# The sum of eight scan results, and x times D, on VectorE instead of GpSimd, under another table of slots

## The chip, the cores and the metric

The kernel runs on one core of a Trainium2 chip. A core has five instruction queues: TensorE (PE in the profile; its weight loads are PEld), VectorE (DVE), ScalarE (ACT), GpSimd (POOL) and SyncE (SP), which here issues nearly all DMA transfers. The metric is device time in microseconds, start to end of one execution; the times given are medians of several runs on the chip. All data is fp32.

## The reference

Eight images of 56 × 56 pixels with 192 channels go through two layers, each with a residual connection.

Layer 0 normalises the image in groups of channels, projects it three times to 576 channels (p, q, v, each through silu), multiplies q by v, convolves the product along rows and along columns with long learned filters, multiplies the sum by p and projects back.

Layer 1 is a two-dimensional selective scan. Cut to what matters:

```
xz = gn(x) @ W_in.T ; xc, z = split(xz)          # 384 + 384 channels
xc = silu(depthwise_conv3x3(xc))
xs = eight orders of the pixels of xc            # K = 8 directions
h[t] = exp(delta[t] * A) * h[t-1] + delta[t] * xs[t] * B[t]     # 16 states a channel
out_y[k] = sum over states of h * C  +  D[k] * xs
y = y0 + y1 + ... + y7                           # each put back into pixel order
y = layernorm(y) * silu(z)
x = x + y @ W_out.T
```

Since D times the input is added for every direction at the same pixel, the kernel adds (sum of the eight D) times xc once per pixel.

## The kernel before

Layer 0 runs first, for all images (its part ends some 3.4 ms into the span). Then layer 1 alternates between a stage that this case calls the stage between images and the scan of one image. The loop `for b in range(-1, B)` has nine such stages: the first only brings image 0 in, the next seven carry image b out and bring image b + 1 in, and the last only carries image 7 out. Eight scans lie between them.

A scan (lines 720 to 1130) is 9600 / 8 = 1200 units of a recurrence over 1024 columns on VectorE (L973), each followed by a multiplication by C on GpSimd (L986) and by transposes on TensorE (L1095) that also sum over the states. The scan's order is written out by hand. Its results go to DRAM, `ytd[b]`, eight results of 384 channels for every pixel; x itself lies in `xrd[b]`.

The stage between images works in tiles of 448 pixels, seven per image. Two streams run in it:

- X, the next image (class `Next`): `load`, `normed` (L458 on VectorE), `project` (L465 on TensorE, L486 on ScalarE), `conv` in three parts (nine taps for three blocks of channels; block 1 on TensorE with diagonal weights, L501, blocks 0 and 2 on VectorE, L505 for the first tap and L503 for the rest), `silu` (L513, ScalarE), `turn` and `away` (transposes and a store of x by pixel), `rows` (L527 on TensorE: the projections that the scan needs, stored by L541), `half` (copies of x into the other orders). For two of the four groups of rows the projection reads the image by columns, so it needs the whole image; those are stream C and come after the last tile of X.
- Y, the image that was scanned (class `Tile`): `load`, `pairs`, `total`, `root`, `scales`, `scaled`, `turn_back`, `normed`, `gate`, `gated`, `finish`. A tile has four parts of 112 pixels. Their inputs are brought ahead by `load_y` (stream L): `yr`, the first four results, `yc`, the other four, and `xty`, x; six buffers each. `pairs(i)` multiplies x by the summed D (L600) and adds the last four results to the first four (L601). `total(i)` adds on: four to two (L608), two to one (L609), plus x times D (L610), and takes the statistics (L611, L612). `root`, `scales`, `scaled` finish the layer norm on ScalarE and VectorE (L616, L620, L622, L628), `turn_back` transposes to channels by rows (L641, L646), `gate` projects z and applies silu (L465, L662), `gated` multiplies (L665), `finish` projects by W_out (L671), adds the residual (L678) and stores (L679).

The order is given by the table PROGRAM. For each step s the table is gone through; an entry such as `('Y', 1, 'scaled')` does that method of tile s − 1 − lag, where the Y stream runs 4 steps later than X (`LAG`), so that X's first four tiles are begun alone. This is the order in which the program names the instructions, and with it their priority. In this stage no order is written out by hand: the framework's planner lays the instructions of each engine by their priorities, its own estimate of durations and when their inputs are due. In the trace VectorE's order therefore departs from the table's. Once laid, each engine's queue is in order, and SyncE's too: a store that is not ready holds the loads behind it.

Of the kernel before, what the change touches and what calls it, by code (L numbers as in the profile page):

```python
# [40 lines left out]
ALU = mybir.AluOpType  # L41
# [5 lines left out]
L = HW * HW  # L47
C = 192
# [23 lines left out]
NR = 5  # L72
AHEAD = 12
LAG = 4
PROGRAM = [('Y', 2, 'gated'), ('Y', 1, 'root'), ('L', 0, '', 1), ('X', 0, 'normed'), ('C', 2, 'rows', 0, 3), ('X', 2, 'conv', 0), ('X', 0, 'project'), ('Y', 1, 'scales'), ('X', 2, 'conv', 1), ('X', 2, 'conv', 2), ('X', 3, 'turn'), ('L', 0, '', 2), ('Y', 0, 'pairs', 1), ('Y', 2, 'finish'), ('Y', 0, 'pairs', 2), ('Y', 1, 'scaled'), ('Y', 0, 'pairs', 0), ('X', 3, 'away'), ('Y', -1, 'pairs', 3), ('Y', 1, 'turn_back'), ('X', 3, 'half', 0), ('Y', 0, 'total', 3), ('Y', 0, 'load'), ('Y', 0, 'total', 1), ('Y', 0, 'normed'), ('C', 2, 'rows', 1, 3), ('L', 0, '', 0), ('Y', 0, 'total', 2), ('X', 3, 'rows', 0), ('Y', 0, 'total', 0), ('C', 2, 'rows', 1, 2), ('X', 3, 'rows', 1), ('L', 1, '', 3), ('Y', 1, 'gate'), ('X', 4, 'half', 1), ('X', -3, 'load'), ('C', 2, 'rows', 0, 2), ('X', 2, 'silu')]
SIZES = (8, 8, 8, 8, 8, 8, 2)
assert sum(SIZES) == NC

# [14 lines left out]
def conv_kernel(ctx: ExitStack, tc: tile.TileContext, a: dict, out: bass.AP):  # L93
    nc = tc.nc
# [337 lines left out]
    for b in range(-1, B):  # L432
        with ExitStack() as st:
# [18 lines left out]
            if norm:  # L452
                wout = one.tile([128, NB, C], F32, name="wout")
                dsb = one.tile([J, DI], F32, name="dsb")
# [128 lines left out]
            class Tile:  # L583
# [9 lines left out]
                def pairs(self, i):  # L593
                    if i == 0:
                        self.st = wk.tile([J, 4, 6], F32, name="yst")
                        self.mv = wk.tile([J, 4, 2], F32, name="ymv")
                        self.yk = {}
                    j = 4 * self.t + i
                    yk, yc, xt = yks[j]
                    nc.gpsimd.tensor_tensor(xt, xt, dsb, ALU.mult)  # L600
                    nc.gpsimd.tensor_tensor(yk[:, 0:4], yk[:, 0:4], yc, ALU.add)  # L601

                def total(self, i):
                    j = 4 * self.t + i
# [78 lines left out]
            X = [Next(t) for t in range(NT)] if more else []  # L683
            Y = [Tile(t) for t in range(NT)] if norm else []
# [18 lines left out]
            for s in range(NT + 12):  # L703
                for stream, late, name, *args in PROGRAM:
                    t = s - late
# [510 lines left out]
```

## Time and profile before

| | |
|---|---|
| median of 3 runs | 28777.4 us (28766.57 to 28782.69) |
| profiled execution | 28792.29 us, span 28790.5 us |
| busy in the span: PE, DVE, ACT, POOL | 26720.9, 25230.4, 21866.3, 22107.1 us |
| stages that carry out and bring in, seven of them | 376.0 to 384.4 us each |
| first stage (in only), last stage (out only) | 226.2 us, 254.1 us |
| DVE busy, POOL busy in the second of the seven | 269.5, 176.3 us |
| L601 on POOL, whole run | 224 times, 905.0 us busy |

A row of the groups gives line, engine, operation, names and shapes, count, busy time, mean duration of one in ns, and the idle time of that engine just before it. A row of the view by source line gives the shortest, median and longest duration in ns. A row of the waits gives who waited for whom, the total in us, how often, and the longest. A row of the timeline gives start and duration in us. Windows are in us from the start of the span. Busy time on an engine is the time from an instruction's start to its end, whatever it did in between.

### The profile page before, as it was taken

The numbers are of one execution on the slowest core, as the hardware profiler recorded it, in microseconds if no ns is written. First come the engines' busy times: TensorE is split into PE (matmuls) and PEld (weight loads), VectorE is DVE, ScalarE is ACT, GpSimd is POOL, SyncE is SP. The second block draws the span as 40 slices with busy tenths as digits, with TensorE's granted clock in tenths as the row PEclk, the third lists the DMA queues.
The fourth block names the chain that finished last, engine by engine and source line by source line (L and its number), as shares of the span: only waits on it lengthen the run. The fifth ranks groups of instructions, "written<-read, shape, count | busy, mean of one in ns | idle before, by whom it ended". The sixth has DMA issues, their size and how long they took to land. (4 is left out here: it accounts for less than half of the span.)

```text
span 28790.5 us, 459134 instructions
## 1 busy us (share of the span) xinstructions
PE 26720.9 (93%) x148912; PEld 15134.0 (53%) x148912; DVE 25230.4 (88%) x16084; ACT 21866.3 (76%) x58050; POOL 22107.1 (77%) x10384
## 2 busy tenths in 40 slices
PE   7999999998999899989999899989998999989997
PEld 4555555554555455544555455545555455545554
DVE  3444489998999899998999899989999899989998
ACT  2333288986998588867889588858997688858886
POOL 0000089987999699987999699979998799969998
PEclk9999999999999999999999999999999999999998
DMA  4222266666666676666666666666666766667666
GB/s 99 57 54 64 62 174 170 171 170 188 172 172 171 174 184 170 171 173 184 173 172 171 182 177 170 172 177 180 171 174 167 190 171 171 171 174 184 170 173 176
DMA packets 5889181, 4641.39 MB, mean 161 GB/s; under 512 B 3814944, under 2 KB 5216000, under 8 KB 5878336
## 3 DMA queue, kind: packets, MB, share of 16 engines
q1 hardware_dynamic: 5853632, 4604.79, 62.1%
q8 instruction: 1189, 19.48, 0.3%
q10 hardware_dynamic: 33152, 7.23, 0.2%
q14 instruction: 1208, 9.90, 0.1%
HBM read 3848.20 MB, written 911.76 MB: 165 GB/s over the span
## 5 line engine op out<-in xcount | busy, mean ns | idle before, releaser
L986 POOL TENSOR_TENSOR hc<-h,cbt 128x1008 f32<-128x1008 f32 x9600 | 20579.1, 2165 | 1708.0 <-DVE h L973 1249.0
L973 DVE TENSOR_TENSOR_SCAN h<-da,bx 128x1024 f32<-128x1024 f32 x9600 | 21122.8, 2264 | 523.3 <-ACT bx L969 492.4
L937 ACT ACTIVATE da<-delta,A_logs 128x252 f32<-128x252 f32 (+1 forms) x39936 | 16821.6, 488 | 771.4 <-DVE h L973 765.6
L958 PE MATMUL bx<-bd,dus 63*128 63x504 f32 x19200 | 10567.5, 635 | 404.5 <-DVE h L973 403.2
L958 PE MATMUL bx<-bd,dut 63*128 63x504 f32 x19200 | 10566.7, 635 | 352.0 <-DVE h L973 328.8
L1095 PEld LDWEIGHTS yps<-ident,hc 128*126 128x126 f32 x76800 | 8311.6, 140 | 3790.2 <-issue 3436.3
L1095 PE MATMUL yps<-ident,hc 128*126 128x128 f32 x76800 | 9449.9, 276 | 210.5 <-POOL hc L986 160.6
L958 PEld LDWEIGHTS bx<-bd,dus 63*128 63x128 f32 x19200 | 2876.6, 186 | 2149.6 <-DVE h L973 1348.6
L958 PEld LDWEIGHTS bx<-bd,dut 63*128 63x128 f32 x19200 | 2876.5, 186 | 2087.4 <-DVE h L973 1234.4
L451 POOL MEMSET xp<- 128x58 f32 x96 | 10.4, 196 | 3417.4 <-DMA x1d<-acc 3417.0
L969 ACT COPY bx<-h 128x16 f32<-128x16 f32 x9408 | 1631.3, 173 | 1081.8 <-PE bx L958 1014.0
L601 POOL TENSOR_TENSOR yr<-yr,yc 112x1536 f32<-112x1536 f32 x224 | 905.0, 4040 | 864.9 <-DMA yc<-yt 547.7
L810 PE MATMUL pd<-dt,dtw 13*128 13x504 f32 x2304 | 1311.6, 649 | 121.9 <-DMA dt<-pxd 41.6
L1122 ACT COPY yt<-yps 126x256 f32<-126x256 f32 x2400 | 859.0, 358 | 579.3 <-PE yps L1095 556.8
L849 PEld LDWEIGHTS pt<-ident,delta 128*128 128x128 f32 x4800 | 503.0, 142 | 1242.3 <-issue 1004.4
L857 DVE TENSOR_TENSOR dut<-pt,xt 128x384 f32<-128x384 f32 x1600 | 850.3, 531 | 337.1 <-DMA bd<-bd 153.9
L849 PE MATMUL pt<-ident,delta 128*128 128x128 f32 x4800 | 886.5, 294 | 34.7 <-ACT delta L825 27.9
L810 PEld LDWEIGHTS pd<-dt,dtw 13*128 13x128 f32 x2304 | 344.7, 187 | 1004.8 <-issue 523.2
L261 ACT ACTIVATE q<-pp,q_b 128x448 f32<-128x448 f32 (+1 forms) x280 | 177.3, 633 | 900.3 <-PE pp L257 900.3
L527 PE MATMUL mm<-xp,pxw 128*128 128x448 f32 x1344 | 823.4, 760 | 0.0
L503 DVE SCALAR_TENSOR_TENSOR acc<-xp,conv_w,acc 128x448 f32<-128x448 f32 x896 | 769.5, 908 | 12.9 <-ACT xp L486 10.5
L319 DVE TENSOR_TENSOR acc<-acc,po 96x896 f32<-96x896 f32 x280 | 303.3, 1083 | 522.3 <-PE po L312 521.8
(126 smaller groups left out, 15384.3 us busy)
## 6 DMA issues: line engine op xcount, KB each, us to landing
cbt<-cd SPq DMA_DIRECT2D x1536, 1008.0 KB
bd<-bd SPq DMA_DIRECT2D x3200, 256.0 KB
dus<-dut SPq DMA_DIRECT2D x3200, 96.0 KB
yt<-ys SPq DMA_DIRECT2D x256, 1176.0 KB
xt<-xt SPq DMA_DIRECT2D x3104, 96.0 KB
ys<-yt SPq DMA_DIRECT2D x9408, 31.5 KB
yr<-yt SPq DMA_DIRECT2D x224, 672.0 KB
yc<-yt SPq DMA_DIRECT2D x224, 672.0 KB
```

The lines of the kernel that those rows point to most:

```text
L527: nc.tensor.matmul(ps, pxw[:, d, g], x[:, t * RT : (t + 1) * RT], start=(d == 0), stop=(d == NB - 1),)
L601: nc.gpsimd.tensor_tensor(yk[:, 0:4], yk[:, 0:4], yc, ALU.add)
L810: nc.tensor.matmul(self.pd[:, : self.n], weights[self.k][:, d * 128 : (d + 1) * 128], self.dt, start=True, stop=True,)
L849: nc.tensor.transpose(self.pt[:, d * 128 : (d + 1) * 128], self.delta[:, d, first : first + 2].rearrange("p c t -> p (c t)"), ident,)
L857: nc.vector.tensor_mul(dut, self.pt[:, :DI], self.xt[p])
L937: yield nc.scalar.activation(da[:, : self.nc, n, 1:], src, AF.Exp, scale=an[:, G.k, self.d, n : n + 1],)
L958: nc.tensor.matmul(self.bx[:, r, :, 1:], G.dut[p][q ^ r ^ int(G.rev)][rows, self.d * 128 : (self.d + 1) * 128], G.bd[p][rows, q, :, :W], s ...
L969: nc.scalar.copy(self.bx.rearrange("p r n t -> p (r n) t")[:, :, 0], src)
L973: nc.vector.tensor_tensor_scan(self.h.rearrange("p n t -> p (n t)"), das[self.P.buf][:, self.slot].rearrange("p n t -> p (n t)"), self.bx. ...
L986: nc.gpsimd.tensor_tensor(hc, h, self.G.cb[self.c // 2][:, :, q * W : (q + 1) * W], ALU.mult)
L1095: nc.tensor.matmul(yps[:, t // 4 % 2, t // 2 % 2], lhsT=hcs[t // 2][:, n].rearrange("p c t -> p (c t)"), rhs=ident, start=(n == 0), stop=( ...
L1122: nc.scalar.copy(y, yps[:, s // 4 % 2])
```

## The change

The two instructions of `pairs` are issued on VectorE instead of GpSimd, with the same operands:

```
-                    nc.gpsimd.tensor_tensor(xt, xt, dsb, ALU.mult)
-                    nc.gpsimd.tensor_tensor(yk[:, 0:4], yk[:, 0:4], yc, ALU.add)
+                    nc.vector.tensor_mul(xt, xt, dsb)
+                    nc.vector.tensor_add(yk[:, 0:4], yk[:, 0:4], yc)
```

After it GpSimd has nothing to do between images but a few memsets.

The table PROGRAM has the same 38 entries with the same delays, in another order:

```
-PROGRAM = [('Y', 2, 'gated'), ('Y', 1, 'root'), ('L', 0, '', 1), ('X', 0, 'normed'), ('C', 2, 'rows', 0, 3), ('X', 2, 'conv', 0), ('X', 0, 'project'), ('Y', 1, 'scales'), ('X', 2, 'conv', 1), ('X', 2, 'conv', 2), ('X', 3, 'turn'), ('L', 0, '', 2), ('Y', 0, 'pairs', 1), ('Y', 2, 'finish'), ('Y', 0, 'pairs', 2), ('Y', 1, 'scaled'), ('Y', 0, 'pairs', 0), ('X', 3, 'away'), ('Y', -1, 'pairs', 3), ('Y', 1, 'turn_back'), ('X', 3, 'half', 0), ('Y', 0, 'total', 3), ('Y', 0, 'load'), ('Y', 0, 'total', 1), ('Y', 0, 'normed'), ('C', 2, 'rows', 1, 3), ('L', 0, '', 0), ('Y', 0, 'total', 2), ('X', 3, 'rows', 0), ('Y', 0, 'total', 0), ('C', 2, 'rows', 1, 2), ('X', 3, 'rows', 1), ('L', 1, '', 3), ('Y', 1, 'gate'), ('X', 4, 'half', 1), ('X', -3, 'load'), ('C', 2, 'rows', 0, 2), ('X', 2, 'silu')]
+PROGRAM = [('X', 0, 'normed'), ('Y', 2, 'gated'), ('X', 2, 'conv', 0), ('X', 0, 'project'), ('C', 2, 'rows', 0, 3), ('Y', 0, 'pairs', 1), ('Y', 1, 'root'), ('X', 2, 'conv', 1), ('X', 3, 'turn'), ('Y', 1, 'scales'), ('X', 2, 'conv', 2), ('Y', 2, 'finish'), ('X', 3, 'away'), ('X', 2, 'silu'), ('L', 0, '', 2), ('Y', 0, 'pairs', 2), ('L', 0, '', 1), ('Y', 0, 'pairs', 0), ('Y', 0, 'total', 1), ('Y', 1, 'scaled'), ('Y', 1, 'turn_back'), ('Y', 0, 'load'), ('L', 0, '', 0), ('Y', 0, 'total', 3), ('Y', 0, 'total', 2), ('Y', -1, 'pairs', 3), ('C', 2, 'rows', 1, 3), ('X', 3, 'rows', 0), ('X', 3, 'rows', 1), ('C', 2, 'rows', 1, 2), ('Y', 1, 'gate'), ('Y', 0, 'total', 0), ('C', 2, 'rows', 0, 2), ('X', 3, 'half', 0), ('L', 1, '', 3), ('X', 4, 'half', 1), ('X', -3, 'load'), ('Y', 0, 'normed')]
```

`nc.vector.tensor_mul` and `tensor_add` are the two-operand product and sum on VectorE, as used in `total`. Line numbers do not move: L600 and L601 are the same two statements before and after.

## The prediction

> **What bounds the kernel now.** The page's slices first: VectorE is lowest, and TensorE stays high, wherever two scans meet, once per image. The windows then split one of these stages, the second of the seven that carry one image out and the next one in, at the end of the last scan, the first convolution, the last convolution, the end of the last projection, and the first scan. Columns: stretch and length, then busy us and instruction count of TensorE, its weight loads, VectorE, ScalarE, GpSimd; the granted TensorE clock; DMA share; GB/s.
>
> ```profile
> 9590.40:9612.00 21.60, 3.00 (x20) 2.36 (x18) 5.24 (x11) 0.74 (x2) 3.41 (x13) 0.58 0.82 257
> 9612.00:9785.10 173.10, 130.63 (x355) 66.32 (x356) 169.09 (x220) 57.41 (x106) 96.86 (x29) 0.85 0.68 186
> 9785.10:9940.00 154.90, 148.47 (x361) 59.65 (x359) 93.60 (x108) 60.23 (x112) 70.93 (x28) 0.98 0.71 215
> 9940.00:9968.20 28.20, 15.52 (x27) 5.10 (x27) 1.60 (x4) 16.98 (x36) 5.09 (x13) 0.58 0.57 112
> ```
>
> Part A (173.1 us) is VectorE's: 169.1 busy, TensorE idle 42.5. Part B (154.9) is TensorE's: idle 6.4, VectorE idle 61. The first and last pieces, 50 us, are loads and the way into the scan; the change touches neither. GpSimd bounds no part.
>
> Next, what VectorE does in A. The groups of that stage (count, busy us, mean ns, idle before):
>
> ```profile
> L503 DVE SCALAR_TENSOR_TENSOR acc<-xp,conv_w,acc 128x448 f32<-128x448 f32 x112 | 102.1, 961 | 0.2
> L608 DVE TENSOR_TENSOR yr<-yr 112x768 f32<-112x768 f32 x28 | 39.6, 1418 | 0.0
> ...
> L505 DVE TENSOR_SCALAR acc<-xp,conv_w 128x448 f32<-128x448 f32 x14 | 11.2, 817 | 1.4 <-ACT xp L486 1.4
> ```
>
> The same convolution line runs in the very first stage too, where there is no image to carry out and no GpSimd add (min/median/max ns, from the view by source line), and there it never waits:
>
> ```profile
> L503 DVE SCALAR_TENSOR_TENSOR acc<-xp,conv_w,acc x112: 670/678/686, 3444.7 to 3534.4; 128x448 f32<-128x448 f32 x112
> L505 DVE TENSOR_SCALAR acc<-xp,conv_w x14: 439/446/453, 3444.3 to 3527.0; 128x448 f32<-128x448 f32 x14
> ```
>
> And the timeline of the middle stage shows what stretches it: a 0.68 us step that starts 0.25 us after a GpSimd add ends with it, and a GpSimd multiply of usually 1.37 us that lasts 17.48 while VectorE runs its steps back to back.
>
> ```profile
> 9618.46 3.50 POOL L601 TENSOR_TENSOR yr<-yr,yc 112x1536 f32<-112x1536 f32 x1 [24.55 <-DMA xty<-xr]
> 9618.71 3.73 DVE L503 SCALAR_TENSOR_TENSOR acc<-xp,conv_w,acc 128x448 f32<-128x448 f32 x1
> ...
> 9640.85 17.48 POOL L600 TENSOR_TENSOR xty<-xty,dsb 112x384 f32<-112x384 f32 x1
> ```
>
> So each engine stands while the other holds something. "Busy" on VectorE in A holds waiting.
>
> **The waiting that goes.** In A, busy less count times the unblocked duration: L503 112 × (961 − 678) ns = 31.7 us; L505 14 × (817 − 446) = 5.2; L608 19.5 busy for 14, less 14 × 0.942 = 6.3; L610 10.0 for 13, less 13 × 0.546 = 2.9; L609 8.2 for 14, less 14 × 0.543 = 0.6; L458 12.6 for 17, less 17 × 0.504 = 4.1. Sum 51 us of 173. The same sum in B (L608 6.9, L609 11.0, L610 8.6, L458 7.3, L622 1.8) gives 36, under TensorE's cover.
>
> **The work that comes.** The multiply has the shape of L609 and L610: 0.56 us. The 112×1536 add has no VectorE row. From 384 to 768 columns (L609 0.557, L608 0.946) the slope is 1.01 ns a column; from 384 to L665's 1344 (1.557) 1.04. That gives 1.72 to 1.76 us; I take 1.74. Together 2.30, and 2.14 in a back-to-back queue, where each record overlaps the next by 0.08. All 28 cost 60 us a stage. On GpSimd the same pairs are busy 112.5 + 56.6 us; that goes and nobody queues for it.
>
> **Rule against row.** The Trainium skill (Perfetto Trace Analysis, Optimizing Scalar/DVE Operations) says that where VectorE is saturated, work may be moved off it, even to GpSimd, and warns that the shared port can spoil this. By its first half the change is wrong: 14 to 17 pairs × 2.14 = 30 to 36 us added to the engine that bounds A, some +230 us over seven stages. The rows answer with the 51 us of standing. The skill's SBUF — State Buffer (Who interferes with whom) states the mechanism: a VectorE instruction with two SBUF inputs, or in a two-port mode, and a GpSimd one that reads SBUF exclude each other whole. L503 and L505 above behave so. I take the rows: −51 + 30 to 36.
>
> **Where it ends.** In A as it stands 14 pairs and 13 totals complete. If the moved pairs keep that pace, A loses 51 − 30 = 21 us; if by the end of the convolution everything the table puts ahead is also done (four tiles and the first pair of the fifth, 17), 51 − 36 = 15. I take 18. Then TensorE, at 130.6 of a 155 us part, has 24 idle instead of 42; it cannot be squeezed evenly, so I let it give back 4. Part B keeps its length: its TensorE work is the same, and its 36 us of VectorE waiting less some 26 for the other 12 pairs was hidden behind 61 us of idleness. So 14 us a stage, 98 for seven.
>
> The first stage has no pairs: 0, with ±5 for the new order. In the last stage, which only carries out, VectorE is 179.5 of 254 busy, of which L609 28 × (1852 − 557) = 36 and L608 and L610 38 more are waiting, plus 44.6 idle at L608 for GpSimd. VectorE's sum alone would fall by 74 + 45 − 60 = 59. But loads there keep the DMA share near 1.0 for 160 us and the first pair waits for its first load: between 0 and 30, nearer the loads' bound: 10.
>
> **The table.** Its slots keep every lag except for order inside a slot: conv and projection of a tile come earlier against the sums, silu moves from the slot's end ahead of them, the normalised x for the gate goes last, pair 3 later. In the trace VectorE's order departs from the table anyway: L608 of the first tile at 9636.1 lies between convolution steps. So the planner that orders this stage will lay it anew. Bounds: from −10 us a stage (silu earlier shortens ScalarE's wait for L503) to +10 (a load behind a store); centre 0. A store does hold loads: SyncE's own waits in A, and GpSimd's, are
>
> ```profile
> SPq L679 <- DVE x L678: 32.5, 1, 32.5
> ...
> POOL yr L601 <- DMA yc<-yt: 39.4, 7, 33.2
> ...
> POOL xty L600 <- DMA xty<-xr: 13.5, 1, 13.5
> ```
>
> The moved queue matters here. GpSimd's waits cost nothing today, since nothing else stands behind them. After the change a pair that waits for its load holds VectorE, and behind it the convolution steps, silu on ScalarE, and then turns and projections on TensorE. SyncE gets no new DMA; its buffer of yc comes free when VectorE, not GpSimd, is through the add.
>
> Sum against the profiled execution (span 28790.5, 28792.3 with what lies around it): −98 − 10 = −108, so 28684. The median of the runs stands 15 lower, 28777.4; the forecast for it is 28669, say 28670.
>
> **Rivals.** *VectorE waits for loads (slower).* The place is A: the 33.2 us wait before the fifteenth pair and the 13.5 us one at the sixth multiply become VectorE's, with convolution behind. 46.7 − 18 = +29 a stage, seven stages and −10: about +190 if both are taken whole; it decides from 18 us a stage on. For it: SyncE's queue is in order and the loads do stand behind an unready store for 32.5 us. Against: that store waits for VectorE itself, which would get to it sooner; and the planner may put late pairs behind the convolution. Half exposed, it is +5 a stage, +25 in all. I take +90 as its middle.
>
> *Hidden anyway (same).* A ends 18 us earlier, but B starts with loads that were issued no earlier, at the DMA share of 0.9 to 1.0 seen in its middle, and the last output tile ends when it did. For it: the last finish (L678) ends only 4 us before the last projection, so the output stream is nearly co-critical. Against: DMA share over A is 0.68, with room to load sooner. It gives 28777 ± 50.
>
> *The change doesn't do what it says:* VectorE could still stand without GpSimd. The first stage's L503, 670 to 686 ns, speaks against that; I leave it no chance of its own.
>
> **How the numbers follow.** Some 0.2% (57 us) is what a measurement of this kernel can tell from no change. The likeliest case (0.55) is 28670, from 28560 (A loses 21, TensorE gives nothing back, the table gives 6, the last stage 30) to 28715. Hidden anyway: 0.15, 28720 to 28830. Loads hold VectorE, or the new order costs as much: 0.30, 28835 to 28970, middle 28870. Leaving about 1 in 10 out at each end gives 28560 to 28890. Faster 0.55, same 0.15, slower 0.30.
>
> **What would show it.** Right: L503 near 0.68 us mean in every stage, L601 on VectorE near 1.74, GpSimd empty between scans; A near 155 us, B near 155. Wrong: idle time of VectorE before L600 or L601 ended by a DMA in A, over 18 us a stage (the slower rival); A shorter and B longer by as much (hidden); L503 still stretched (the lock is not it); an add far above 1.76 us.

## The result, and the profile after

The changed kernel takes 28503.07 us (median, 28486.33 to 28506.23), before 28771.99 in the same comparison: the ratio is 0.9905, 95% interval 0.9889 to 0.992. The direction was forecast; the size, 269 us, is two and a half times the 108 us forecast and lies below the range.

In the profiled executions the span falls from 28790.5 to 28504.0 us, by 286.5. Cut at the stages: the seven that carry out and bring in fall from 379.6 to 341.7 us in the mean, 265 together; the last from 254.1 to 241.2, 13; the part up to the first scan by 6; the eight scans by 2. So the change acts where it was put, and in each of the seven stages it gives 37.9 us instead of 14.

The windows of the changed kernel's second such stage, cut at the same four events as before (start, first projection, last convolution, last projection for the scan, first scan; columns as before):

```profile
9547.70:9569.50 21.80, 2.32 (x20) 1.84 (x18) 5.14 (x12) 0.74 (x2) 3.40 (x13) 0.69 0.81 256
9569.50:9729.50 160.00, 150.76 (x456) 77.34 (x456) 154.63 (x264) 67.44 (x123) 0.00 (x0) 0.97 0.87 239
9729.50:9860.90 131.40, 119.44 (x258) 45.65 (x258) 77.32 (x122) 51.03 (x94) 0.00 (x0) 0.95 0.72 207
9860.90:9888.60 27.70, 15.73 (x27) 5.17 (x27) 1.57 (x3) 16.54 (x34) 5.09 (x13) 0.57 0.53 108
```

Head and tail stay at 22 and 28 us. Part A goes from 173.1 to 160.0, part B from 154.9 to 131.4. VectorE is still full in A, but TensorE, which was idle for 42 of 173 us there, is now idle for 9 of 160, and does 456 matmuls in A instead of 355. Of the 714 matmuls of A and B, 258 instead of 359 are left for B (a row can count a matmul that lies across a cut twice).

VectorE's groups of that stage:

```profile
L503 DVE SCALAR_TENSOR_TENSOR acc<-xp,conv_w,acc 128x448 f32<-128x448 f32 x112 | 68.6, 671 | 0.2
L601 DVE TENSOR_TENSOR yr<-yr,yc 112x1536 f32<-112x1536 f32 x28 | 48.9, 1747 | 1.3 <-DMA yc<-yt 1.3
L608 DVE TENSOR_TENSOR yr<-yr 112x768 f32<-112x768 f32 x28 | 26.1, 941 | 0.0
L600 DVE TENSOR_TENSOR xty<-xty,dsb 112x384 f32<-112x384 f32 x28 | 15.2, 543 | 0.0
```

The convolution step is back at 671 ns from 961, the first sum at 941 from 1418. The add costs 1747 ns, forecast 1740; the multiply 543, forecast 560. And VectorE waits for loads before its pairs for 1.3 us in the whole stage, where GpSimd had waited 74.4 us for yc.

### The profile page after: what moved, and what is told of

It is laid out like the page before. It is cut to its first block, busy times and chain, and to the rows that moved or that the text cites. A ratio compares the mean times of both kernels' runs of the same rounds, so it can differ in the third digit from the quotient of the medians.

```text
span 28504.0 us, 458613 instructions
## 1 busy us (share of the span) xinstructions
PE 26664.6 (94%) x148912; PEld 15113.4 (53%) x148912; DVE 25001.0 (88%) x16532; ACT 21872.4 (77%) x58050; POOL 20753.0 (73%) x9936
## 5 line engine op out<-in xcount | busy, mean ns | idle before, releaser
L527 PE MATMUL mm<-xp,pxw 128*128 128x448 f32 x1344 | 798.9, 745 | 2.4 <-ACT px L539 2.4
L819 ACT COPY delta<-pd 128x504 f32<-128x504 f32 x1152 | 646.1, 561 | 117.2 <-PE pd L810 97.9
```

Source lines behind the costliest of these rows:

```text
L527: nc.tensor.matmul(ps, pxw[:, d, g], x[:, t * RT : (t + 1) * RT], start=(d == 0), stop=(d == NB - 1),)
L819: nc.scalar.copy(self.delta[:, d, :, :W], self.pd[:, : self.n].rearrange("p (c t) -> p c t", t=W))
```

## The experiments

In all of them a stage is cut at the same events; A and B in the text are means over the seven stages, and the rows show the second. For the kernels above A and B are 172.5 and 156.6 before and 158.4 and 132.9 after. An instruction that waits inside its own busy time is said to stand.

### The move or the table

Two parts were changed at once. The first kernel moves the engine under the old table:

```
-                    nc.gpsimd.tensor_tensor(xt, xt, dsb, ALU.mult)
-                    nc.gpsimd.tensor_tensor(yk[:, 0:4], yk[:, 0:4], yc, ALU.add)
+                    nc.vector.tensor_mul(xt, xt, dsb)
+                    nc.vector.tensor_add(yk[:, 0:4], yk[:, 0:4], yc)
```

> The two pair instructions on VectorE under the old table. If the port is the cause (theory P), L503 falls to 0.68 us mean in every stage and the seven stages fall from about 379 to 340-350 us: 200 to 280 us of the 269 in all. If the table's order is the cause (theory T), L503 falls too, but the stages stay within 10 us of 379: less than 80 us in all, the shorter first part being given back in the second.

The second has the new table alone:

```
-PROGRAM = [('Y', 2, 'gated'), ('Y', 1, 'root'), ('L', 0, '', 1), ('X', 0, 'normed'), ...
+PROGRAM = [('X', 0, 'normed'), ('Y', 2, 'gated'), ('X', 2, 'conv', 0), ('X', 0, 'project'), ...
```

> The pairs stay on GpSimd, the new table orders the stage. Theory P: L503 stays near 0.96 us and the seven stages stay at 370 to 385 us, within 60 us of before in all. Theory T: the stages fall by 20 us or more each, 150 us or more in all, with L503 still stretched. If each gives part (both under 200 us), the two act together: the sum of both gains against 269 us says whether they add.

The move alone: 28518.38 us, ratio to before 0.9905 (0.9888 to 0.9922). The table alone: 28824.24 us, 1.0012 (1.0003 to 1.0022), slightly slower than before. The move makes the whole gain: beside the kernel before, measured with it, it saves 270 us, and the whole change 269. What the new order adds to it can't be told from no effect; without it the order costs 36 us. The convolution step of the move alone, then of the table alone:

```profile
L503 DVE SCALAR_TENSOR_TENSOR acc<-xp,conv_w,acc 128x448 f32<-128x448 f32 x112 | 68.8, 677 | 0.2
```

```profile
L503 DVE SCALAR_TENSOR_TENSOR acc<-xp,conv_w,acc 128x448 f32<-128x448 f32 x112 | 103.5, 970 | 0.8 <-ACT xp L486 0.5
```

The windows of parts A and B, in the same order:

```profile
9576.10:9732.70 156.60, 137.57 (x407) 70.99 (x408) 147.92 (x253) 63.34 (x115) 0.00 (x0) 0.91 0.92 252
9732.70:9874.50 141.80, 136.81 (x309) 52.61 (x307) 84.77 (x133) 55.32 (x102) 0.00 (x0) 0.98 0.60 184
```

```profile
9621.00:9795.90 174.90, 137.83 (x382) 69.67 (x382) 170.66 (x220) 59.58 (x109) 97.73 (x30) 0.84 0.69 190
9795.90:9954.50 158.60, 145.52 (x332) 57.68 (x332) 84.23 (x109) 58.11 (x108) 63.57 (x26) 0.96 0.73 203
```

In the mean, the move alone brings A to 153.1 and B to 142.1 us; the table then puts 49 more matmuls into A (456 after 407), and A is 5 us longer and B 9 shorter. In the last stage the table costs something in these profiles: 219.8 us under the old one, 241.2 under the new one.

### Is it the port, or the hand-over?

With the pairs on VectorE two things are gone: GpSimd beside VectorE, and VectorE's waiting for results that GpSimd delivers. This kernel brings back only the first:

```
                     nc.vector.tensor_add(yk[:, 0:4], yk[:, 0:4], yc)
+                    idle = wk.tile([J, 4, DI], F32, name="idle", bufs=1)
+                    nc.gpsimd.tensor_tensor(idle, yc, yc, ALU.add)
```

> The changed kernel, and beside each pair of adds on VectorE a GpSimd add of 1536 columns of yc to itself, into a tile that nobody reads. Nothing waits for it except the buffer of yc. If the two engines exclude each other (theory P), L503 goes back to 0.85-0.95 us mean, the first part of a stage grows by 25-40 us and the time to 28700-28800 us, about that of before. If the gain came from VectorE no longer waiting for GpSimd's results (theory H, the hand-over), L503 stays at 0.67 and the time within 60 us of the changed kernel, 28500-28560.

28844.07 us, 1.0022 (1.0013 to 1.0032) of before: the gain is gone and a little more. Stages of 383.6 us in the mean, A 192.5, B 142.0; the last stage, where the add runs too, takes 278.7. A grows by 34.1 us and VectorE's busy time in it by 34.3. The add also holds the buffer of yc longer, but VectorE waits for no load before its pairs (0.0 in the row of L601 below), so late loads are not the cause. So GpSimd's presence is enough; the hand-over is not needed. The expectation for L503 failed, though. The groups, of VectorE and of GpSimd (from L608 on, line numbers are two higher here: L610 is the sum L608):

```profile
L503 DVE SCALAR_TENSOR_TENSOR acc<-xp,conv_w,acc 128x448 f32<-128x448 f32 x112 | 68.6, 670 | 0.2
L601 DVE TENSOR_TENSOR yr<-yr,yc 112x1536 f32<-112x1536 f32 x28 | 51.4, 1836 | 0.0
L610 DVE TENSOR_TENSOR yr<-yr 112x768 f32<-112x768 f32 x28 | 33.8, 1216 | 0.0
L600 DVE TENSOR_TENSOR xty<-xty,dsb 112x384 f32<-112x384 f32 x28 | 31.4, 1120 | 0.0
...
L458 DVE TENSOR_SCALAR x1n<-x,gstat 96x448 f32<-96x448 f32 x14 | 13.8, 1009 | 0.0
```

```profile
L603 POOL TENSOR_TENSOR idle<-yc 112x1536 f32<-112x1536 f32 x28 | 146.8, 5242 | 159.8 <-DMA yc<-yt 147.7 <-DMA pxd<-px 11.0
```

The standing is carried by the sums, the multiply and the normalisation, and by GpSimd itself (5.24 us in the mean, shortest 2.75, longest 19.81), not by the convolution. It is not that GpSimd's adds fell elsewhere. In the seven stages 24 of the 196 began during an L503; each of these 24 took over 4.5 us, while the longest L503 took 0.69. In the kernel before 66 of 196 began there, only 13 of these took over 4.5 us, and 110 of the 784 L503 took over 0.9. The two adds differ in their operands (yr and yc into yr before, yc twice into a third tile here); why one held the convolution up and the other gave way to it is not shown.

### Does any GpSimd work do it?

```
+                    idle = wk.tile([J, 4, DI], F32, name="idle", bufs=1)
+                    for _ in range(3):
+                        nc.gpsimd.memset(idle, 0.0)
```

> The changed kernel, and beside each pair three GpSimd memsets of 1536 columns (about 1.4 us each), which write the on-chip memory and read none of it. If exclusion needs a GpSimd read against a VectorE step with two inputs (theory P, as the Trainium skill's SBUF page has it), L503, L608 to L610 keep their durations; only the steps with one input in the two-port mode (L505, L458) can be stretched, at most 35 of them a stage: 0-8 us a stage, 28505-28565 us. If any GpSimd work excludes VectorE, the time goes to 28700-28850 as with the add.

28626.68 us, 0.9946 (0.9931 to 0.9961): 123 us of the gain lost, twice the most that was expected. The groups say which steps stand:

```profile
L503 DVE SCALAR_TENSOR_TENSOR acc<-xp,conv_w,acc 128x448 f32<-128x448 f32 x112 | 68.6, 670 | 0.2
L601 DVE TENSOR_TENSOR yr<-yr,yc 112x1536 f32<-112x1536 f32 x28 | 48.9, 1746 | 0.5 <-DMA yc<-yt 0.5
...
L458 DVE TENSOR_SCALAR xnext<-xnext,gstat 96x448 f32<-96x448 f32 x14 | 20.4, 1494 | 15.5 <-DMA xnext<-x1d 15.5
...
L614 DVE BATCH_NORM_STATS2 yst<-ysum 112x6 f32<-112x384 f32 x28 | 14.8, 546 | 0.1
...
L505 DVE TENSOR_SCALAR acc<-xp,conv_w 128x448 f32<-128x448 f32 x14 | 12.4, 901 | 0.0
...
L458 DVE TENSOR_SCALAR x1n<-x,gstat 96x448 f32<-96x448 f32 x14 | 9.3, 688 | 0.0
```

The two-input steps shown are untouched: L503 670 ns, L601 1746, as without memsets. Of the steps with one input the TENSOR_SCALAR ones are stretched: L458 to 1494 and 688 ns from 504 or less, L505 to 901 from 446, against a memset's 1.42 us. The statistics (L611, here L614), with one input too, stay at 546. That is the distinction the Trainium skill draws (SBUF — State Buffer, Who interferes with whom): two SBUF inputs contend only with a GpSimd instruction that reads SBUF, a two-port mode, which TENSOR_SCALAR can enter, with any, and other one-input steps with none. The durations agree with it; which mode a step ran in is not in the trace. The size was missed because the memsets wait for nothing and crowd into A (none is left for B): there the three lines L458 (twice) and L505 stand for 14 × 0.99 + 14 × 0.18 + 14 × 0.46 = 23 us, which make the stage 17.5 us longer.

### Which part pays

The forecast took waiting in B as hidden by VectorE's 61 idle us. The same GpSimd add was put beside the first four tiles only, then beside the last three only, in the seven stages:

```
+                    if more and self.t < 4:       # the other kernel: self.t >= 4
+                        idle = wk.tile([J, 4, DI], F32, name="idle", bufs=1)
+                        nc.gpsimd.tensor_tensor(idle, yc, yc, ALU.add)
```

> The GpSimd add beside the pairs of the first four of the seven output tiles only (most of them run before the last convolution), in the seven stages that carry out and bring in. Add beside all 28 pairs cost 42 us a stage, 34 in the first part and 9 in the second. If waiting in the first part costs nearly whole and waiting in the second is covered by TensorE (the forecast's step), this run bears nearly all of it: 34-42 us a stage, 28740-28800 us.

> The same beside the pairs of the last three output tiles only, which mostly run after the last convolution. If the second part's waiting is covered by TensorE (the forecast's step), the time stays within 25 us of 28503. If it is not covered, each stage grows by 8-12 us, all of it in the second part: 28560-28590 us.

28741.70 us for the first four tiles, 0.9984 (0.9974 to 0.9994); 28572.37 for the last three, 0.9926 (0.9911 to 0.9941). Parts A and B of the one, then of the other:

```profile
9617.00:9811.20 194.20, 158.90 (x456) 80.28 (x456) 189.86 (x264) 67.26 (x124) 100.00 (x16) 0.89 0.73 197
9811.20:9942.70 131.50, 118.28 (x258) 45.08 (x258) 77.30 (x121) 50.85 (x94) 0.00 (x0) 0.95 0.72 206
```

```profile
9592.80:9752.00 159.20, 151.15 (x456) 77.73 (x456) 154.52 (x264) 67.38 (x124) 7.88 (x1) 0.96 0.87 241
9752.00:9894.20 142.20, 121.26 (x258) 46.34 (x258) 101.39 (x121) 51.03 (x94) 40.77 (x12) 0.90 0.68 191
```

Matmul counts are those of the changed kernel, 456 and 258, so work has not moved between the parts, and the two effects separate: in the mean A +34.8 and B −0.6 in the first, A +0.4 and B +9.4 in the second. In A VectorE's busy time grew by 34.9 us, and all of it is paid. In B it grew by 25.0 and 9.4 is paid, although VectorE has 55 us to spare there; TensorE's idle time in B rose from 11.9 to 20.3. The expectation that named 8 to 12 us is the one that held.

### What bounds it now

> The changed kernel without pairs: the last four results and the multiplication by D are left out, their loads stay. It takes 60 us of VectorE work out of each of eight stages. If VectorE still sets the first part after the change, it shortens by 25-35 us and the stages go from 341 to 305-318 us: 28250-28330 us. If TensorE has become the bound (idle 21 us in the 291 us between the first projection and the last), the stages lose at most 15 us each: 28390-28490 us.

This kernel leaves out the two lines of `pairs`, so its output is not the sum. 28376.44 us, 0.9861 (0.9844 to 0.9877), 127 us below the changed kernel, between the two ranges that were expected: the stages fall by 17, to 324.5 us. Its parts A and B:

```profile
9557.10:9681.20 124.10, 121.12 (x376) 63.48 (x377) 118.95 (x227) 61.01 (x110) 0.00 (x0) 0.98 0.94 262
9681.20:9830.10 148.90, 141.85 (x341) 56.10 (x339) 54.67 (x103) 57.58 (x106) 0.00 (x0) 0.99 0.78 221
```

A becomes 34 us shorter (VectorE's busy time in it falls by 36) and B 17.6 longer, with 84 matmuls more in the mean. TensorE is idle for 10 us in A and B together, so without pairs it is TensorE that sets the stage; of the 58 us that pairs take of VectorE in a stage, 17 are still paid in the changed kernel.

### Two small additions

The old table for the last stage, the new one elsewhere (`for ... in PROGRAM if more else LAST`):

> The changed kernel with the old table in the last stage alone, which only carries an image out. If the new table's 241 us there against 220 us under the old one (seen in the run with the engine alone changed) is the table's, the time falls by 15-21 us to 28482-28490 us, faster than both; if it belongs to the state that the stages before leave, it stays at 28503.

28493.36 us, 0.9900 (0.9885 to 0.9915). The last stage took 220.1 us, as under the old table, so that reading held; but the same stage under the new table is not constant (241.2, and 229.5 to 230.7 in three other profiles of it). Measured beside the changed kernel:

> The changed kernel once more, beside the next two: 28495-28510 us.

> The changed kernel with the old table in the last stage, measured beside the changed kernel: 10 to 20 us faster than it, 28480-28495 us, if the last stage's 220 us against 230-241 us holds.

28509.20 (28504.16 to 28517.78) for the changed kernel and 28502.26 (28491.11 to 28504.81) with the old table last: 7 us instead of the 10 to 20 expected, below what this kernel's measurement can tell.

The last addition, made to the kernel with the old table last, concerns TensorE's first matmuls in a stage:

```
+            warm = pm.tile([128, T], F32, name="mm")
+            for _ in range(40):
+                nc.tensor.matmul(warm[:, :128], ident, ident, start=True, stop=True)
```

> The same, and at the start of every stage 40 products of two 128x128 tiles that nobody reads, in the some 20 us in which TensorE waits for the first loads. If matmuls after an idle stretch are slow because the clock was lowered (0.95 us instead of 0.54 for L465, about 18 of them in a stage), most of them become fast and a stage loses 3-6 us: 28440-28475 us. If they are slow for another reason, or VectorE paces the start anyway, the time stays with the run beside it, within 15 us.

28491.72 us, 0.9897 (0.9883 to 0.9912). The fillers ended 8 to 9 us before the first projection, which still had 5 to 9 slow matmuls (4 to 9 without fillers), so this run tells nothing of the cause. With 90 of them:

> As the last, with 90 idle products instead of 40, so that TensorE is occupied until its first load is there (with 40 it stood still again for 9 us before the first projection). If slow matmuls come from the clock after an idle stretch, the first projection of each stage takes 0.54 us a matmul instead of up to 1.11, some 8 slow ones fewer, and a stage loses 2-4 us: 28465-28485 us. If not, the first ones stay slow and the time at 28490-28505 us.

The first 36 matmuls of the stage's first projections (min/median/max ns), in the changed kernel and with 90 fillers (where L465 is L466):

```profile
L465 PE MATMUL mm<-xnext,win x36: 537/539/1112, 9569.5 to 9588.5; 96*128 96x448 f32 x36
```

```profile
L466 PE MATMUL mm<-xnext,win x36: 537/539/543, 9589.2 to 9604.6; 96*128 96x448 f32 x36
```

Five microseconds at the start of these projections, in the changed kernel and with 90 fillers (the granted clock is the third figure from the end):

```profile
9570.00:9575.00 5.00, 5.00 (x8) 2.13 (x8) 3.04 (x7) 0.53 (x1) 0.00 (x0) 0.50 1.03 254
```

```profile
9590.00:9595.00 5.00, 5.00 (x15) 2.58 (x14) 3.26 (x6) 1.60 (x3) 0.00 (x0) 1.00 1.01 260
```

In the changed kernel the granted clock is 0.50 there, with filled idle time it is 1.00, and the nine slow matmuls of this stage are gone. So the slowness is the clock. But the time is 28514.38 us, 0.9903 (0.9887 to 0.992): the fillers held the first projection back from 21.8 to 23.5 us after the scan, its 36 matmuls ended 1.8 us earlier, and A kept its length (158.3 us in the mean), since VectorE is busy for 153.4 of it. The expected gain of 2 to 4 us a stage did not come. Apart from the kernel that leaves the pairs out, no version clearly beats the changed kernel.

## Why the prediction was right and wrong

**The bound and the mechanism: right.** L503 and L505 are at their first-stage durations or just below (671 and 438 ns in the mean after 678 and 446), adding GpSimd work restores the old time, and the price on VectorE was met within 7 ns for the add. One reading was loose: the 3.73 us step of L503 does not end with the GpSimd add but 0.48 us after it. The advice to move work off a full engine (the Trainium skill, Perfetto Trace Analysis, Optimizing Scalar/DVE Operations) pointed the wrong way here in its first half; its own caution about the shared port is what decided.

**The shortening of A: right for the move alone.** Forecast 18, with 21 if 14 pairs and 13 totals end in A. With the move alone exactly 14 and 13 do so, and A is 19.4 us shorter, with VectorE's busy time in it down by 20.7. Under the new table 15 and 15 do, A is 14.1 us shorter, and it contains more of TensorE's work.

**"I let it give back 4": wrong.** TensorE gave nothing back. Its idle time in A fell from 42.9 us to 18.6 with the move alone and to 7.7 with the table. In the stage shown nearly all of it was waiting for ScalarE, and ScalarE's silu was waiting for the convolution; before:

```profile
PE turn L550 <- ACT xt L555: 14.5, 2, 10.2
PE yt L641 <- ACT y L646: 12.7, 1, 12.7
PE mm L465 <- ACT sz L662: 8.8, 1, 8.8
```

```profile
ACT xp L513 <- DVE acc L503: 51.4, 7, 15.5
```

and ScalarE after:

```profile
ACT xp L513 <- DVE acc L503: 5.3, 4, 1.9
```

None of TensorE's three waits is left in A after the change. That they went with VectorE's standing, by way of ScalarE, fits these rows; it was not tried by itself.

**"Part B keeps its length: its TensorE work is the same": this is the step that failed.** B is 14.5 us shorter with the move alone and 23.7 after. Its TensorE work is not the same: of 714 matmuls 359 are left for B before, 307 with the move alone and 258 after, and TensorE's busy time in B falls from 149.0 to 137.2 and 121.0 us. With the move alone that makes 11.8 of the 14.5 us. After, it makes 28.0, of which 4.3 are lost again because TensorE is idle for 11.9 us in B instead of 7.6. The work went into the idle time that the forecast had left to TensorE in A: of the 101 matmuls, 47 belong to the output stream and 54 to the next image (convolution 18, rows 24, turns 12). Work moved into A is not enough by itself: with the table alone 27 more lie there, and B is 3.3 us longer, with TensorE idle for 13.3. Why the planner lays more into A when the pairs are on VectorE is not shown.

Two smaller terms belong to the same step. TensorE's busy time in A and B together fell by 7 us a stage (278.6 to 271.7): there are fewer matmuls of 0.95 us, 33 to 22 among those of L465, L501 and L671 and 91 to 84 of L527, and the granted clock in A of the stage shown rose from 0.85 to 0.97. And the forecast took the 36 us of VectorE's waiting in B as hidden. In the kernel before that was nearly so: with the same work B could not have lost more than TensorE's idle 7.6 us, and with the move alone it lost 2.7 of them. In the changed kernel it no longer holds: put back, 9.4 of 25.0 us are paid. Idle time of VectorE summed over a part does not cover a wait that TensorE's next matmul depends on; which chain passes it on was not traced.

Counted on TensorE, A and B became 37.8 us shorter: 30.9 of idle time and 6.9 of busy time, where the forecast had 18 less 4.

**The table: 0 ± 10 us a stage forecast.** Beside the move it is −4.7 a stage, and +21 in the last one in the profile taken. Taken apart from the move it costs 5.7 a stage.

**The last stage: 10 forecast, between 0 and 30.** 34 with the move alone, above that range; 13 and 23 in two profiles of the changed kernel. The loads bound it less than was taken: of the 59 us that VectorE's sum alone would have given, 34 came under the old table. They did hold VectorE, though, and more under the new table. The move alone, then the changed kernel:

```profile
DVE yr L601 <- DMA xty<-xr: 22.8, 1, 22.8
...
DVE yr L601 <- DMA yc<-yt: 11.6, 10, 2.0
```

```profile
DVE yr L601 <- DMA yc<-yt: 37.2, 20, 3.7
DVE yr L601 <- DMA xty<-xr: 23.2, 1, 23.2
```

**The slower rival: did not occur in the seven stages.** VectorE waits for loads before pairs for 1.3 us in the one shown and at most 2.8 in any; only in the last stage, just shown, are such waits long. SyncE still waits for the store's input (L678), 40.9 us in the stage after 38.7, but 18.0 at the longest instead of 32.5, and the loads of the fifteenth pair were issued at 137 us of the stage instead of 182. **Hidden anyway:** the output stream moved with the rest.

## What to carry to other kernels

A VectorE row whose mean is far above its shortest can be a wait inside the busy time; look for the same line and shape in a stretch without GpSimd work, and price a move by that row, not by the mean. An addition to a full engine can then be cheaper than its neighbour's use of a shared resource. And when an engine's waits in one part go, don't stop at that part: the planner may lay later work into the gap, and then the next part gets shorter too. Count the work that is left there; idle time of one engine is cover only for work that the bounding engine does not wait for.

## What the runs showed of the hardware

A GpSimd add of 1536 columns whose shortest record is 3.42 us stretched VectorE steps of 0.5 to 0.9 us to 3.7 to 4.2. An add of the same size that reads one tile twice was itself held up to 19.81 us by a row of VectorE steps, and a multiply 17.48; no turn after a fixed time is seen. GpSimd memsets left L503, L601 and the statistics at their durations and stretched the TENSOR_SCALAR steps (L458 from 504 to 1494 ns, L505 from 446 to 901). After the 16 to 18 us in which TensorE is idle at a stage's start, the clock was granted at 0.50 to 0.62 for the first 5 us, and 4 to 9 fp32 matmuls of 448 columns took 0.9 to 1.1 us before the rest ran at 0.54; 8 to 9 us of idleness after fillers were enough to bring that back.
